# Attention after a scan layer: one copy of q and k for maxima and scores, two heads on the halves of the array, a written order per engine, projections in a stage of their own

## The chip, the cores and the metric

One Trainium2 chip, one core. The metric is device time in microseconds: 4778.94 us as the median of three runs of the kernel before (4752.04 to 4829.39).

## What is computed

Two layers over x of shape 8 x 1024 x 256 (batch, position, width), all in float32. The first is a selective scan with a gated convolution, followed by a layer norm. The second is attention with 16 heads of 16 channels plus a mixture of eight experts with the best two kept, followed by a layer norm. The change touches the attention alone.

```python
qkv = (x @ W_qkv + b_qkv).reshape(B, S, 3, H, hd)
q, k, v = (qkv[:, :, 0], qkv[:, :, 1], qkv[:, :, 2])
attn = jnp.einsum('bqhd,bkhd->bhqk', q, k) / jnp.sqrt(jnp.asarray(hd, x.dtype))
attn = jax.nn.softmax(attn, axis=-1)
attn_out = jnp.einsum('bhqk,bkhd->bqhd', attn, v).reshape(B, S, D)
...
return attn_out + moe_out
```

## The kernel before

`scan_moe_layer` does the whole first layer and the experts of the second. It leaves, per batch, the sum of x and the experts' part in DRAM (`acc`) and the transposed x (`x2T`). `attention_layer` then does the attention, batch by batch, in pairs of heads: 8 batches of 8 pairs, 64 pairs.

*Projections.* `prep(b, o)` (L596 on) projects one batch. Each block of 128 channels by 512 positions of q or k (`pq`, L614) is split into a high part, rounded to float32r by ACT (L619), and a low part by DVE (L620). Both go to DRAM (`qk`, L625), each block in two DMAs, so that q lies as (high, low, high, low) and k as (high, high, low, low): the product of 64 such rows is the full product of 16 channels. V goes to `vaug` (L634, L639) with a column of ones after each head. `prep(0)` runs before the loop; the following batches' preparations are generators whose pieces the loop puts between its own work.

*Maxima.* A softmax wants the maximum of every query's scores first. `maxima` (L664 to L703) multiplies with the queries as output rows: for each of 8 query tiles and 2 halves of the keys, two matmuls of 64 rows, one per head on each half of the array (`sm`, L689), then one DVE reduction over 1024 columns (L693). At the end of a pair, `insert` (L667 to L678) transposes the negated maxima (`pm`), splits them into high and low (L671, L672), and four small DMAs write them as two rows under q in `qst` (L675).

*Scores.* `score(n)` (L706 on) multiplies with the keys as output rows, 66 rows deep: 64 rows of k and two rows of ones meet 64 rows of q and the two rows of maxima, so the maximum is subtracted inside the product. One score tile is one head, 128 keys and 1024 queries: two matmuls (`sc`, L714), then one exponential of 1024 columns by ACT (L716). So q and k of a pair are loaded twice, into `qmx`, `kmx` for the maxima and `qst`, `kst` for the scores (L656, L662), in rings of three.

*Weighing.* `weigh(n)` (L720 on) multiplies V with the exponentials of two score tiles, four heads-by-halves side by side on strips of 32 columns (`av`, L733). After the last one ACT copies the result (L739); `collect` transposes it back (L747), divides by the sum of weights (L751, L754) and POOL adds it to `acc` (L758). `normalize` does the last layer norm of a batch on DVE (L765 to L776), the power on POOL (L772).

*Order.* TensorE (PE), ACT, DVE and POOL follow the order in which the program is written; SP, which issues the DMAs, is not among them. The loop at the end of `attention_layer` makes one step of maxima, a weighing in every second turn and one score tile per turn; the maxima run 24 steps (`LEAD`) ahead, 16 steps being a pair. Score and maxima tiles share three buffers of 1024 columns in PSUM, `ps_s`; the projections, transposes and the like have one, `ps_m`.

Of the kernel before, what the change touches and what calls it, by code (L numbers as in the profile page):

```python
# [47 lines left out]

# [475 lines left out]
@with_exitstack  # L534
def attention_layer(ctx, tc, ident, acc_in, x2T, w_qkv, b_qk, b_v, out):

# [10 lines left out]
    RING = 3  # L556
    LEAD = 24
    TILES = 2 * NT
    PIECES = 24
    VW = HD + 1  # L560

    wp = ctx.enter_context(tc.tile_pool(name="a_w", bufs=1))
    p1 = ctx.enter_context(tc.tile_pool(name="a_1", bufs=1))
    p2 = ctx.enter_context(tc.tile_pool(name="a_2", bufs=2))
    p3 = ctx.enter_context(tc.tile_pool(name="a_3", bufs=3))
    p5 = ctx.enter_context(tc.tile_pool(name="a_5", bufs=5))
    ps_s = ctx.enter_context(tc.tile_pool(name="a_pss", bufs=3, space=PSUM))
    ps_a = ctx.enter_context(tc.tile_pool(name="a_psa", bufs=1, space=PSUM))
    ps_m = ctx.enter_context(tc.tile_pool(name="a_psm", bufs=1, space=PSUM))
    dp = ctx.enter_context(tc.tile_pool(name="a_dram", bufs=2, space=DRAM))  # L570
# [8 lines left out]
    nc.gpsimd.memset(half, -0.5)  # L579

    vaug = []
    for i in range(2):
        t = wp.tile([P, NT, NH * VW + 32 - VW], F32, name=f"vaug{i}")
        nc.gpsimd.memset(t, 1.0)
        vaug.append(t)

    qmx, kmx, qst, kst = [], [], [], []
    for i in range(RING):
        qmx.append(wp.tile([P, S], F32R, name=f"qmx{i}"))
        kmx.append(wp.tile([P, S], F32R, name=f"kmx{i}"))  # L590
        qst.append(wp.tile([KS + 2, 2, S], F32R, name=f"qst{i}"))
        t = wp.tile([KS + 2, 2, S], F32R, name=f"kst{i}")
        nc.gpsimd.memset(t[KS : KS + 2].bitcast(F32), 1.0)
        kst.append(t)

    def prep(b, o):  # L596

        acc = p2.tile([P, NT, H], F32, tag="acc", name=f"acc_{b}")
        nc.sync.dma_start(acc, acc_in[b].rearrange("(t p) h -> p t h", p=P))
        o["acc"] = acc  # L600
        xT = p2.tile([P, HK, S], F32, tag="xT", name=f"axT_{b}")
        nc.sync.dma_start(xT, x2T[b])
        yield
        yield

        o["d"] = []
        for c in range(H // P):
            d = dp.tile([2, P, 2, 2, S], F32, tag=f"qk{c}", name=f"qk_{b}_{c}")
            o["d"].append(d)
            for a in range(2):  # L610
                for q in range(NQ):
                    pq = ps_m.tile([P, QB], F32, tag="mm", name=f"pq_{b}_{c}_{a}_{q}")
                    for k in range(HK):
                        nc.tensor.matmul(  # L614
                            pq, wr[:, k, a * H + c * P : a * H + (c + 1) * P], xT[:, k, q * QB : (q + 1) * QB],
                            start=(k == 0), stop=(k == HK - 1),
                        )
                    hl = p3.tile([P, 2, QB], F32R, tag="hl", name=f"hl_{b}_{c}_{a}_{q}")
                    nc.scalar.activation(hl[:, 0, :], pq, AF.Identity, bias=bqk[:, a, c : c + 1])  # L619
                    nc.vector.scalar_tensor_tensor(  # L620
                        hl[:, 1, :], pq, bqk[:, a, c : c + 1], hl[:, 0, :].bitcast(F32), ALU.add, ALU.subtract
                    )
                    for i in range(2):
                        dst = d[a, :, :, i, :] if a == 0 else d[a, :, i, :, :]
                        nc.sync.dma_start(dst[:, :, q * QB : (q + 1) * QB], hl.bitcast(F32))  # L625
                    yield
        va = vaug[b % 2]
        o["v"] = va
        for t2 in range(NT // 2):
            pv = ps_m.tile([P, 2, H], F32, tag="mm", name=f"pv_{b}_{t2}")  # L630
            for j in range(2):
                t = 2 * t2 + j
                for k in range(HK):
                    nc.tensor.matmul(  # L634
                        pv[:, j, :], xT[:, k, t * P : (t + 1) * P], wr[:, k, 2 * H :],
                        start=(k == 0), stop=(k == HK - 1),
                    )
            for j in range(2):
                nc.vector.tensor_add(  # L639
                    va[:, 2 * t2 + j, 0 : NH * VW].rearrange("p (h d) -> p h d", d=VW)[:, :, 0:HD],  # L640
                    pv[:, j, :].rearrange("p (h d) -> p h d", d=HD), bv.rearrange("p (h d) -> p h d", d=HD),
                )
            yield

    pairs = [(b, p) for b in range(NB) for p in range(NP)]
    work = [{} for _ in range(NB)]

    def rows_of(i, a):
        b, p = pairs[i]
        c, r = divmod(2 * p, HC)  # L650
        return work[b]["d"][c][a, HD * r : HD * r + 2 * HD].rearrange("d i j s -> (d i j) s")

    def load_max(i):
        if i < len(pairs):
            for a, t in ((0, qmx[i % RING]), (1, kmx[i % RING])):
                nc.sync.dma_start(t.bitcast(F32), rows_of(i, a))  # L656

    def load_pair(i):
        if i < len(pairs):
            for a, t in ((0, qst[i % RING]), (1, kst[i % RING])):  # L660
                for hh in range(2):
                    nc.sync.dma_start(t[0:KS, hh, :].bitcast(F32), rows_of(i, a)[KS * hh : KS * hh + KS])  # L662

    def maxima():  # L664


        def insert(i, mn):  # L667
            pt = ps_m.tile([P, P], F32, tag="mm", name=f"pm_{i}")
            nc.tensor.transpose(pt[:TILES, :], mn, ident)
            mr = p2.tile([TILES, 2, P], F32R, tag="mr", name=f"mr_{i}")  # L670
            nc.scalar.copy(mr[:, 0, :], pt[:TILES, :])  # L671
            nc.vector.tensor_sub(mr[:, 1, :], pt[:TILES, :], mr[:, 0, :].bitcast(F32))  # L672
            for hh in range(2):
                for l in range(2):
                    nc.sync.dma_start(  # L675
                        qst[i % RING][KS + l : KS + l + 1, hh, :].bitcast(F32),
                        mr[hh * NT : (hh + 1) * NT, l, :].bitcast(F32),
                    )  # L678

        mn = None  # L680
        for i, (b, p) in enumerate(pairs):
            qt_, kt_ = qmx[i % RING], kmx[i % RING]
            mh = p2.tile([P, 2, NT, NQ], F32, tag="mh", name=f"mh_{b}_{p}")
            for t in range(NT):
                for kh in range(NQ):
                    s = ps_s.tile([P, 2, QB], F32, tag="s", name=f"sm_{b}_{p}_{t}_{kh}")
# [7 lines left out]
                    if i and t == 1 and kh == 0:  # L694
                        insert(i - 1, mn)
# [5 lines left out]
        insert(i, mn)  # L701
        yield

    live = {}

    def score(n):  # L706

# [171 lines left out]
```

## Time and profile before

| | |
|---|---|
| median of the runs | 4778.94 us |
| runs | 4752.04 to 4829.39 us |
| profiled execution, span from first to last instruction | 4713.3 us |
| busy: PE, DVE, ACT, POOL | 4031.4, 3296.9, 2322.1, 1940.1 us |
| granted TensorE clock, mean | 0.896 |
| first projection of the attention | 2603.5 us |
| first exponential, last exponential | 2670.7, 4693.0 us |
| DMA | 454.6 MB, 96 GB/s |

Times are microseconds from the first instruction unless they are durations. PE is TensorE's matmuls, PEld its weight loads, DVE VectorE, ACT ScalarE, POOL GpSimd, SP the engine that issues DMAs. L693 is line 693 of the kernel. In a group, `out<-in` are the program's names, then the shape, the count, busy time and mean nanoseconds of one, and the engine's idle time before it with what ended most of it. A float32 matmul has two records, a float32r one has one. The profiled execution's own time outside its span isn't recorded; the median of the runs is 65.6 us above the span, the shortest run 38.7.

### The profile page before, as it was taken

To read this page: it belongs to the slowest core of one execution; us is meant where nothing else is said; L and a number is where in the kernel's file an instruction comes from. 1 tells how busy PE (TensorE), PEld (TensorE's weight loads), DVE (VectorE), ACT (ScalarE), POOL (GpSimd) and SP (SyncE) were. 2 spreads that over 40 slices of the span, in tenths; PEclk is the share of its full clock that TensorE was granted. 3 is DMA by queue.
4 is the path that set the end of the run, shared out by engine and by line. 5 is a ranking of instruction groups with operands and counts; after the bars stand their busy time and mean duration, and the time that the engine had idled before them with its cause. 6 is when DMAs were issued, how large, how long until landed. Compare 5 with 4: busy or idle time off the path is not lost.

```text
span 4713.3 us, 43473 instructions
## 1 busy us (share of the span) xinstructions
PE 4031.4 (86%) x15168; PEld 1528.1 (32%) x15168; DVE 3296.9 (70%) x3774; ACT 2322.1 (49%) x3178; POOL 1940.1 (41%) x664
## 2 busy tenths in 40 slices
PE   7688787887888878878766799999999999999998
PEld 2233332332233323333222233333333333333333
DVE  4777787677777777777783467567676666776765
ACT  4545444554455444534430156456565455555555
POOL 4978777787777776877781000000000000000000
PEclk8788898898988988899878799699999798998989
DMA  5433334333333433433321542243434242423321
GB/s 139 103 93 89 77 92 99 83 95 74 99 86 90 91 84 85 108 77 84 87 58 45 168 142 79 90 126 106 137 90 144 63 152 73 143 82 117 108 72 28
DMA packets 188621, 454.58 MB, mean 96 GB/s; under 512 B 25882, under 2 KB 63410, under 8 KB 187378
## 3 DMA queue, kind: packets, MB, share of 16 engines
q1 hardware_dynamic: 188402, 451.80, 35.4%
q8 instruction: 120, 1.97, 0.2%
q14 instruction: 99, 0.81, 0.1%
HBM read 323.78 MB, written 126.88 MB: 96 GB/s over the span
## 4 chain that ended last, share of the span: by engine, by line
PE 56%; DVE 17%; ACT 11%; POOL 6%; issue 4%; DMA 1%; ACTq 0%; POOLq 0%; SPq 0%; DVEq 0%
PE sc L714 12%; PE av L733 11%; PE pe L386 8%; PE sm L689 7%; ACT es L716 7%; DVE dz L493 6%; PE pc L191 5%; DVE x L394 5%; POOL dz L445 3%; DVE dz L438 3%; PE pq L614 2%; POOL dz L440 2%; PE pr L240 2%; PE y L455 1%; PE po L283 1%
## 5 line engine op out<-in xcount | busy, mean ns | idle before, releaser
L693 DVE TENSOR_REDUCE mh<-sm 128x2 f32<-128x1024 f32 x1024 | 1243.2, 1222 | 380.2 <-PE sm L689 372.0
L716 ACT ACTIVATE es<-sc 128x1024 f32<-128x1024 f32 x1024 | 1047.0, 1024 | 810.3 <-PE sc L714 783.8
L445 POOL TENSOR_TENSOR dz<-dz,ct 128x2048 f32<-128x2048 f32 x256 | 1156.6, 4524 | 504.1 <-DVE dz L493 264.3
L428 ACT ACTIVATE da<-ex,am 128x512 f32<-128x512 f32 x1024 | 700.0, 689 | 945.6 <-DVE dz L493 926.6
L714 PE MATMUL sc<-qst,kst 66*128 66x512 f32 x2048 | 796.9, 473 | 41.2 <-ACT es L716 36.4
L758 POOL TENSOR_TENSOR acc<-acc,ot 128x256 f32<-128x256 f32 x64 | 46.7, 729 | 1842.8 <-DVE ot L754 1720.8
L386 PE MATMUL pe<-we,yT 128*128 128x512 f32 x1024 | 528.2, 640 | 217.4 <-DVE x L394 214.2
L493 DVE TENSOR_TENSOR_SCAN dz<-da,state,dz 128x512 f32<-128x512 f32 x512 | 629.5, 1268 | 88.5 <-ACT da L428 87.3
L493 DVE TENSOR_TENSOR_SCAN dz<-da,dz 128x512 f32<-128x512 f32 x512 | 596.6, 1206 | 56.9 <-ACT da L428 56.6
L440 POOL TENSOR_TENSOR dz<-ex,bt 128x2048 f32<-128x2048 f32 x128 | 591.6, 4622 | 24.6 <-DMA ex<-dl 22.8
L733 PE MATMUL av<-es,vaug 128*32 128x512 f32 x4096 | 589.5, 649 | 0.0
L689 PE MATMUL sm<-kmx,qmx 64*128 64x512 f32 x2048 | 544.3, 528 | 29.1 <-DVE mh L693 7.7
L714 PEld LDWEIGHTS sc<-qst,kst 66*128 66x128 f32 x2048 | 325.6, 200 | 647.8 <-DVE mh L693 262.5
L394 DVE SCALAR_TENSOR_TENSOR x<-pe,gcb,x 128x256 f32<-128x256 f32 x512 | 246.4, 481 | 274.7 <-PE pe L386 265.5
L386 PEld LDWEIGHTS pe<-we,yT 128*128 128x128 f32 x1024 | 180.9, 195 | 547.3 <-issue 526.7
L689 PEld LDWEIGHTS sm<-kmx,qmx 64*128 64x128 f32 x2048 | 201.8, 194 | 458.9 <-ACT es L716 215.9
L455 PE MATMUL y<-dz,sl 128*32 128x512 f32 x2048 | 307.8, 677 | 42.7 <-POOL dz L445 42.7
L438 DVE TENSOR_TENSOR dz<-ex,pb 128x2048 f32<-128x2048 f32 x128 | 289.6, 2263 | 55.0 <-DMA ex<-dl 55.0
L191 PE MATMUL pc<-hs,dw 128*128 128x512 f32 x512 | 260.5, 646 | 45.2 <-POOL hs L182 45.2
L254 PE MATMUL pb<-xd,rp 16*128 16x512 f32 x256 | 154.7, 685 | 105.6 <-DVE dz L438 70.0
L171 PE MATMUL ph<-xT,wi 128*128 128x512 f32 x256 | 171.1, 807 | 63.3 <-DVE x L301 45.5
L240 PE MATMUL pr<-xT,wi 128*128 128x512 f32 x256 | 144.5, 715 | 32.3 <-ACT du L230 29.8
(104 smaller groups left out, 2816.7 us busy)
## 6 DMA issues: line engine op xcount, KB each, us to landing
ex<-dl SPq DMA_DIRECT2D x256, 512.0 KB
qk<-hl SPq DMA_DIRECT2D x128, 512.0 KB
dl<-du SPq DMA_DIRECT2D x64, 512.0 KB
qmx<-qk SPq DMA_DIRECT2D x64, 512.0 KB
kmx<-qk SPq DMA_DIRECT2D x64, 512.0 KB
qst<-qk SPq DMA_DIRECT2D x128, 256.0 KB
kst<-qk SPq DMA_DIRECT2D x128, 256.0 KB
ct<-bc SPq DMA_DIRECT2D x256, 64.0 KB
```

Of the source, the lines that this page charges most:

```text
L191: nc.tensor.matmul(pc, dw[:, c0 + j, k, :], hss[j][:, k : k + LT], start=(k == 0), stop=(k == KC - 1))
L386: nc.tensor.matmul(pe.rearrange("p e f -> p (e f)"), yT[:, k, t * P : (t + 1) * P], we[:, k, 2 * e2 : 2 * e2 + 2, :].rearrange("p e f -> p ...
L394: nc.vector.scalar_tensor_tensor(xt[:, t, :], pe[:, j, :], cb[:, t, e : e + 1], xt[:, t, :], ALU.mult, ALU.add)
L428: nc.scalar.activation(da, o["ex", c][:, r, 0, :], AF.Exp, scale=am[:, c, g, r : r + 1])
L440: nc.gpsimd.tensor_mul(t, o["ex", c][:, :, 1, :], o["bt", g].unsqueeze(1).to_broadcast(full))
L445: nc.gpsimd.tensor_mul(t, t, o["ct", g].unsqueeze(1).to_broadcast([P, NR, LT]))
L493: nc.vector.tensor_tensor_scan(t[:, r, :], da, t[:, r, :], 0.0 if steps[i][1] == 0 else state[:, c, g, r : r + 1], ALU.mult, ALU.add,)
L689: nc.tensor.matmul(s[:, hh, :], qt_[rows, t * P : (t + 1) * P], kt_[rows, kh * QB : (kh + 1) * QB], start=True, stop=True,)
L693: nc.vector.tensor_reduce(mh[:, :, t, kh], s, AX.X, ALU.max)
L714: nc.tensor.matmul(s[:, cols], kt_[:, hh, kt * P : (kt + 1) * P], qt_[:, hh, cols], start=True, stop=True)
L716: nc.scalar.activation(e, s, AF.Exp, scale=HD**-0.5)
L733: nc.tensor.matmul(av[32 * j : 32 * j + 32, :], va[:, kt, VW * h : VW * h + 32], es[hh][:, q * QB : (q + 1) * QB], start=(kt == 0), stop=( ...
```

## The change

One copy of q and of k per pair, `q4` and `k4` of 128 rows with one head on each half, serves maxima and scores alike, and each is loaded once. A score tile is now both heads for 128 keys and 512 queries: two matmuls of 64 rows on the halves, and then two more that add the maxima, `ones` (two rows of ones in each half, zeros elsewhere) against `mrow` (the two rows of maxima in each half, zeros elsewhere). A maxima tile has two buffers of one bank, each reduced by a DVE instruction of its own over 512 columns. DRAM holds q and k once (high and low); the copies arise in the loads.

The order is no longer a loop of generators. Every piece of work is a task with an engine, a duration that the plan assumes and a place `v` in that engine's order; one unit of `v` holds one tile of 128 queries of the maxima and one of 128 keys of the scores. On each engine the tasks are emitted sorted by `v`; the plan's clock decides buffers and the order on SP, which is now among the engines that follow the written order. Within a unit TensorE has, by `v`: the weighing, a maxima tile, two score tiles, a maxima tile. Once per pair the transposes of an older pair (`back`) and of the maxima (`turn`) stand between the two score tiles and share one score buffer. The maxima are 11 units ahead of the scores (`LEAD`), 8 units being a pair. PSUM buffers: two score tiles (`R_s`), three single banks for maxima and projections (`R_d`), one for the weighing.

All projections, in half batches, get places below zero, ahead of all pairs. Last, `normalize` scales on POOL, except for six of eight tiles of the last batch.

```diff
+class Plan:
+    ENGINES = ("PE", "ACT", "DVE", "POOL")
+    TAIL = {"PE": 0.3, "DVE": 0.17, "ACT": 0.2, "POOL": 0.12, "SP": 0.0}
+    SWITCH = 0.2
...
+    def add(self, eng, us, fn, v, reads=(), writes=(), mode=None):
+        t = Task()
+        t.eng, t.us, t.fn, t.v, t.mode = eng, us, fn, v, mode
+        t.tail = self.TAIL[eng]
...
+    def run(self):
+        from collections import deque
+        queue = {e: deque(sorted((t for t in self.tasks if t.eng == e), key=lambda t: (t.v, t.n))) for e in self.ENGINES}
+        sp = [t for t in self.tasks if t.eng == "SP" and not t.left]
+        free = dict.fromkeys(self.ENGINES + ("SP",), 0.0)
...
+            for t in [q[0] for q in queue.values() if q] + sp:
+                if t.left:
+                    continue
+                at = max(free[t.eng], t.ready)
+                taken = []
+                for b in t.new:
+                    if b.slot is None:
+                        j = b.pool.find(taken)
+                        if j is None:
+                            break
+                        at = max(at, b.pool.free[j])
+                        taken.append((b.pool, j))
+                else:
+                    if best is None or (at, t.v, t.n) < best[:3]:
+                        best = (at, t.v, t.n, t)
...
+            if e == "SP":
+                sp.remove(t)
+                free[e] = at + 0.06
+                dma = max(dma, at + 0.06) + t.us
+                t.end = dma + 2.0
+            else:
+                queue[e].popleft()
+                us = t.us
+                if e == "PE" and t.mode != mode:
+                    us += self.SWITCH
+                    mode = t.mode
+                free[e] = at + us
+                t.end = at + us + t.tail
+            t.fn()
...
-    RING = 3
-    LEAD = 24
-    TILES = 2 * NT
-    PIECES = 24
+    LEAD = NT + 3
+    LATE = 2
     VW = HD + 1
+    VR = NH * VW + 32 - VW
+    plan = Plan()
...
+    ones_in = wp.tile([P, P], F32, name="ones_in")
+    nc.sync.dma_start(ones_in, ones2)
+    ones = wp.tile([P, P], F32R, name="ones")
+    nc.scalar.copy(ones, ones_in)
+    R_v = ring("vaug", NB, [P, NT, VR])
+    for t in R_v.tiles:
         nc.gpsimd.memset(t, 1.0)
-        vaug.append(t)
-    qmx, kmx, qst, kst = [], [], [], []
-    for i in range(RING):
-        qmx.append(wp.tile([P, S], F32R, name=f"qmx{i}"))
-        kmx.append(wp.tile([P, S], F32R, name=f"kmx{i}"))
-        qst.append(wp.tile([KS + 2, 2, S], F32R, name=f"qst{i}"))
-        t = wp.tile([KS + 2, 2, S], F32R, name=f"kst{i}")
-        nc.gpsimd.memset(t[KS : KS + 2].bitcast(F32), 1.0)
-        kst.append(t)
-    def prep(b, o):
-        o["d"] = []
+    R_q = ring("q4_", 3, [P, S], F32R)
+    R_k = ring("k4_", 3, [P, S], F32R)
+    R_m = ring("mrow", 2, [P, S], F32R)
+    for t in R_m.tiles:
+        nc.gpsimd.memset(t.bitcast(F32), 0.0)
+    R_s = ring("s", 2, [P, 2, QB], pool=pp)
+    R_d = ring("d", 3, [P, QB], pool=pp)
+    R_av = ring("av", 1, [P, QB], pool=pp)
+    R_es = ring("es", 10, [P, 2, QB])
+    R_x = ring("axT", 2, [P, HK, QB])
+    R_avs = ring("avs", 2, [P, QB])
+    R_hl = ring("hl", 4, [P, 2, QB], F32R)
+    R_acc = ring("acc", 2, [P, NT, H])
+    R_mh = ring("mh", 2, [P, 2, NT, NQ])
+    R_mn = ring("mn", 2, [P, 2 * NT])
...
+    def prep(b, q, v0):
+        o, xT, n = work[b], Buf(R_x), 0
+        def load():
+            nc.sync.dma_start(xT.t, x2T[b][:, :, q * QB : (q + 1) * QB])
+        plan.add("SP", 3.0, load, v0 - 2, writes=[xT])
+                pq, hl = Buf(R_d), Buf(R_hl)
+                def proj(pq=pq, c=c, a=a):
                     for k in range(HK):
                         nc.tensor.matmul(
-                            pq, wr[:, k, a * H + c * P : a * H + (c + 1) * P], xT[:, k, q * QB : (q + 1) * QB],
+                            pq.t, wr[:, k, a * H + c * P : a * H + (c + 1) * P], xT.t[:, k],
                             start=(k == 0), stop=(k == HK - 1),
                         )
-                    hl = p3.tile([P, 2, QB], F32R, tag="hl", name=f"hl_{b}_{c}_{a}_{q}")
-                    nc.scalar.activation(hl[:, 0, :], pq, AF.Identity, bias=bqk[:, a, c : c + 1])
...
+                plan.add("PE", 1.71, proj, v, reads=[xT], writes=[pq], mode="f")
+                plan.add("ACT", 0.6, high, v, reads=[pq], writes=[hl])
+                plan.add("DVE", 0.65, low, v + 0.05, reads=[pq, hl], writes=[hl])
+                def store(hl=hl, c=c, a=a):
+                    nc.sync.dma_start(
+                        o["d"][c][a, :, :, q * QB : (q + 1) * QB].rearrange("i p s -> p i s"), hl.t.bitcast(F32)
+                    )
+                plan.add("SP", 2.5, store, v, reads=[hl], writes=[o["dbuf"][c]])
+        for t2 in range(TQ // 2):
+            v = v0 + 0.1 * n
+            n += 1
+            pv = Buf(R_d)
...
+            plan.add("PE", 1.71, projv, v, reads=[xT], writes=[pv], mode="f")
+            plan.add("DVE", 0.65, addv, v + 0.05, reads=[pv], writes=[o["v"]])
...
+        v0 = NT * i
+        q4, k4, mrow = Buf(R_q), Buf(R_k), Buf(R_m)
+        for a, t in ((1, k4), (0, q4)):
+            for hh in range(2):
+                def load(a=a, t=t, hh=hh):
+                    heads = o["d"][c][a, :, HD * (r + hh) : HD * (r + hh + 1)]
+                        dst = t.t[KS * hh + 2 * HD * i : KS * hh + 2 * HD * (i + 1)].bitcast(F32)
+                        src = heads if a == 0 else heads[i : i + 1].to_broadcast([2, HD, S])
+                        nc.sync.dma_start(dst, src)
+                plan.add("SP", 1.5, load, v0 - 4, reads=[o["dbuf"][c]], writes=[t])
+        mh, mn, mr = Buf(R_mh), Buf(R_mn), Buf(R_mr)
+        for t in range(NT):
+            for kh in range(NQ):
+                s = [Buf(R_d), Buf(R_d)]
+                v = v0 + t + (0.2, 0.8)[kh]
+                def mx(s=s, t=t, kh=kh):
                     for hh in range(2):
                         rows = slice(KS * hh, KS * hh + KS)
                         nc.tensor.matmul(
-                            s[:, hh, :], qt_[rows, t * P : (t + 1) * P], kt_[rows, kh * QB : (kh + 1) * QB],
+                            s[hh].t, q4.t[rows, t * P : (t + 1) * P], k4.t[rows, kh * QB : (kh + 1) * QB],
-                    nc.vector.tensor_reduce(mh[:, :, t, kh], s, AX.X, ALU.max)
-                    if i and t == 1 and kh == 0:
-                        insert(i - 1, mn)
-                    yield
-            mn = p2.tile([P, TILES], F32, tag="mn", name=f"mn_{b}_{p}")
-            nc.vector.tensor_reduce(mn.rearrange("p (h t) -> p h t", h=2), mh, AX.X, ALU.max, negate=True)
-            load_max(i + RING)
-        yield
...
+                    plan.add("DVE", 0.585, red, v, reads=[s[hh]], writes=[mh])
+        v = v0 + NT
+        pm = Buf(part_of=seam.setdefault(i, Buf(R_s)))
...
+        def turn():
+            nc.tensor.transpose(pm.t[: 2 * NT, 0, 0:P], mn.t, ident)
...
+        plan.add("DVE", 0.1, neg, v - 0.1, reads=[mh], writes=[mn])
+        plan.add("PE", 0.12, turn, v + 1.51, reads=[mn], writes=[pm], mode="f")
+        plan.add("ACT", 0.2, high, v + 1.52, reads=[pm], writes=[mr])
+        plan.add("DVE", 0.2, low, v + 1.21, reads=[pm, mr], writes=[mr])
+        for hh in range(2):
+            for l in range(2):
+                def row(hh=hh, l=l):
+                    nc.sync.dma_start(
+                        mrow.t[KS * hh + l : KS * hh + l + 1, :].bitcast(F32),
+                        mr.t[hh * NT : (hh + 1) * NT, l, :].bitcast(F32),
+                    )
+                plan.add("SP", 0.05, row, v, reads=[mr], writes=[mrow])
+        av = Buf(R_av)
+        for kt in range(NT):
+            es = []
+            for q in range(NQ):
+                s, e = Buf(R_s), Buf(R_es)
+                es.append(e)
+                v = v0 + LEAD + kt + (0.4, 0.6)[q]
+                cols = slice(q * QB, (q + 1) * QB)
+                def score(s=s, kt=kt, cols=cols):
+                    for hh in range(2):
+                        rows = slice(KS * hh, KS * hh + KS)
+                        nc.tensor.matmul(
+                            s.t[:, hh, :], k4.t[rows, kt * P : (kt + 1) * P], q4.t[rows, cols], start=True, stop=False
+                        )
+                    for hh in range(2):
+                        rows = slice(KS * hh, KS * hh + KS)
+                        nc.tensor.matmul(s.t[:, hh, :], ones[rows, :], mrow.t[rows, cols], start=False, stop=True)
...
+                plan.add("PE", 0.43, score, v, reads=[q4, k4, mrow], writes=[s], mode="h")
+                plan.add("ACT", 0.93, exp, v, reads=[s], writes=[e])
...
+            plan.add(
+                "PE", 0.92, weigh, v0 + LEAD + kt + LATE, reads=[o["v"], *es, *([av] if kt else [])],
+                writes=[av], mode="c",
+            )
+        v = v0 + LEAD + NT - 1 + LATE
+        avs, pt, rc, ot = Buf(R_avs), Buf(part_of=seam.setdefault(i + 3, Buf(R_s))), Buf(R_rc), Buf(R_ot)
+        w = v0 + 4 * NT
...
+        plan.add("ACT", 0.5, out_av, v + 0.35, reads=[av], writes=[avs])
+        plan.add("PE", 0.45, back, w + 1.5, reads=[avs], writes=[pt], mode="f")
+        plan.add("DVE", 0.2, recip, w + 1.22, reads=[pt], writes=[rc])
...
+            plan.add("DVE", 0.22, scale, w + 1.23, reads=[pt, rc], writes=[ot])
...
+            def norm(t=t):
+                eng = nc.vector if last and t % 4 else nc.gpsimd
+                eng.tensor_scalar(
+                    acc.t[:, t, :], acc.t[:, t, :], mv.t[:, t, 0:1], rs.t[:, t : t + 1], ALU.subtract, ALU.mult
+                )
+            plan.add("DVE" if last and t % 4 else "POOL", 0.7, norm, v0 + gap * (NT + t), reads=[mv, rs, acc], writes=[acc])
...
+            prep(b, q, NQ * b + q - 20)
+    for b in range(NB):
+        load_acc(b)
+        for p in range(NP):
+            pair(b * NP + p)
+        normalize(b)
-    with tc.manual_schedule(engines={eng.PE, eng.Activation, eng.DVE, eng.Pool}):
-        mx = maxima()
-        for _ in range(LEAD):
-            step(mx)
-        gens, due = [], 0.0
...
-            step(mx)
-            if n % 2 == 0 and 0 <= n - 4 < ALL:
-                weigh(n - 4)
-            if n < ALL:
-                score(n)
...
+    with tc.manual_schedule(engines={eng.PE, eng.Activation, eng.DVE, eng.Pool, eng.SP}):
+        plan.run()
```

## The prediction

> **What bounds the kernel now.** I read the page's busy times and slices first, then its groups by line, then the timeline of a quiet stretch, then the busy times by window. A unit below means two maxima tiles, two score tiles and one weighing; 8 units make a pair of heads, and there are 64 pairs.
>
> ```profile
> span 4713.3 us, 43473 instructions
> PE   7688787887888878878766799999999999999998
> PEclk8788898898988988899878799699999798998989
> L693 DVE TENSOR_REDUCE mh<-sm 128x2 f32<-128x1024 f32 x1024 | 1243.2, 1222 | 380.2 <-PE sm L689 372.0
> L716 ACT ACTIVATE es<-sc 128x1024 f32<-128x1024 f32 x1024 | 1047.0, 1024 | 810.3 <-PE sc L714 783.8
> ```
>
> The attention is the right half of the slices: from about 2600 us on TensorE is at 9 in nearly every one. The maxima (DVE, L693) and the exponentials (ACT, L716) idle, both because of TensorE. The timeline shows one unit, start to start:
>
> ```profile
> 3404.30 0.73 PE L714 MATMUL sc<-qst,kst 66*128 66x512 f32 x2
> 3405.11 0.51 PE L689 MATMUL sm<-kmx,qmx 64*128 64x512 f32 x2
> 3405.55 1.07 PE L733 MATMUL av<-es,vaug 128*32 128x512 f32 x8
> 3406.55 0.73 PE L714 MATMUL sc<-qst,kst 66*128 66x512 f32 x2
> 3407.21 0.50 PE L689 MATMUL sm<-kmx,qmx 64*128 64x512 f32 x2
> 3407.64 0.73 PE L714 MATMUL sc<-qst,kst 66*128 66x512 f32 x2
> ```
>
> Score 0.81 (0.15 of it a wait for an exponential's buffer), maxima 0.44, weighing 1.00, score 0.66, maxima 0.43: 3.34 us. The single records at full clock give the same, as medians: a maxima pair 0.425, a score tile 0.337 + 0.326, a weighing 0.453 + 0.542, together 3.17. How much of that is streaming? A 512-column pass takes 0.2155 (a projection of V, two passes of 256 columns per record, repeats every 0.2155; Q and K records every 0.428). So a maxima pair, whose two matmuls start 2 ns apart, streams 0.21 and loses 0.21; a score tile streams 0.43 and loses 0.23; the weighing streams 0.853 and loses 0.14. Five visits lose 1.04 us of 3.34.
>
> A clean pair takes 27.2 us, yet the 64 take 2022 (4693 less 2671), 31.6 each. The rest is projections put in between, and the clock:
>
> ```profile
> 2604.00:2648.00 44.00, 27.62 (x78) 12.54 (x76) 14.02 (x21) 5.50 (x8) 2.68 (x2) 0.97 0.80 270
> 2648.00:2671.00 23.00, 16.29 (x43) 6.05 (x41) 22.96 (x23) 0.59 (x2) 0.00 (x0) 0.50 0.79 213
> 2671.00:2706.00 35.00, 34.70 (x93) 11.58 (x91) 15.59 (x15) 13.17 (x14) 0.00 (x0) 0.50 0.09 32
> 2948.00:3020.00 72.00, 72.00 (x211) 23.68 (x211) 34.61 (x41) 27.11 (x29) 2.39 (x2) 0.50 0.16 44
> 3020.00:3700.00 680.00, 649.31 (x3138) 248.61 (x3138) 489.15 (x573) 395.94 (x423) 20.09 (x25) 1.00 0.39 122
> ```
>
> The columns after the length are PE, PEld, DVE, ACT and POOL, then the clock, the DMA share and GB/s. Some stretches run at a clock of 0.50 though TensorE never rests; 284 us between 2671 and 4693 do, and a unit is 6.46 there.
>
> **The change, part by part.** (1) *One mode for maxima and scores.* A score tile becomes two pairs of half-height matmuls (the scores, then the row of ones against the maxima), each pair as wide as a maxima pair. Streaming does not shrink: 4 passes before, 4 after. What falls is visits: the written order is weighing, maxima, score, score, maxima, so two visits instead of five. Six pairs in a row cost 0.2155 each at best and 0.235 by the closest row (three maxima pairs in a row at 2641.39 come 0.338 and 0.235 apart, the first with its entry); I take 0.22, since the trace's last units put four score matmuls in a row into 1.13 us, which leaves 0.225 each after 0.23 for the visit. Unit: 6 x 0.22 + 0.23 entry and exit + 0.995 = 2.55 (2.52 to 2.64). The 0.15 wait goes: ACT needs 2 x 1.03 of 2.55.
>
> (2) *Maxima per bank.* Each 1024-wide reduction becomes two of 512. Back to back the wide one repeats every 1.137 us (14 in 15.92 from 2645.09). No 512-wide reduction is in the trace: half of it is 0.57, and the 128x512 additions record 0.67. Records overlap by 0.09 (1.222 against 1.137), so I take 0.60, nearest to the addition less that overlap. DVE per unit: 2.40 (2.27 to 2.68), under the 2.55 of TensorE but close.
>
> The Trainium skill (TensorEngine Tiling (Array Packing), Performance Considerations) speaks against the change here: tiling speeds up TensorE and not the emptying of PSUM. By that rule with the upper price, 2.68, DVE would set the unit and a pair would be 24.7; by the row it does not.
>
> (3) *The seam of each pair.* Transposes, which were spread out, now stand together once per pair between two score tiles: four at 0.108, an exit of 0.20, the turn of the maxima 0.21 and one more entry and exit of the half mode 0.23, about 1.0 us on TensorE. They take one of two score buffers. By hand, with the durations above: from the start of the unit the first score ends at 1.8, the transposes at 2.65; ACT is free for the copy of the maxima at 3.1; the second score waits for the first exponential until 3.15, the next weighing starts at 4.05. So a seam costs 1.5. DVE, behind that copy, runs the correction, reciprocal and two scalings until 4.45 and is level again one unit later. Queued behind it are the reductions of the second maxima tile, and TensorE waits for these only through three banks, which just suffices.
>
> (4) *Maxima rows by DMA.* From seam start: the first copy ends at 3.4 and the second at 3.65, four issues of 0.64 on SP follow; at 3303.04 to 3307.13 first issue to last packet took 4.1. That makes 7.5; the ones pass needs the rows at 8.1, three units of lead instead of the four before. 0.6 to spare, nothing in the sum beyond the 0.6 below. If SP is in the middle of the next pair's eight loads (0.5 each), the rows are 3.4 to 5 late.
>
> (5) *Loads.* 1 MB a pair instead of 2, eight issues of 0.5 against six: SP is off the path. Nothing gained; these lay beside TensorE.
>
> (6) *Projections in their own stage.* Per half batch 4 x 1.71 + 2 x 1.72 = 10.3, sixteen times 164.6, plus 1.7 for a first window at half clock and 4 for edges: 170. With three buffers for a chain of 3.6 us (1.71, then 0.3, 0.69, 0.75 and waits) TensorE keeps going; with one, as before, the cadence was 3.55 and the stage 320, the upper bound. The moved DMAs are 64 stores of 512 KB (32 us of SP issue) and 16 loads: 42 MB, which at the 270 GB/s of the window above is 155 us, under 165; at 213 GB/s it is 197 and the stage 27 longer. All pair loads now queue on SP behind these stores, which costs the first pair alone, and its data are ready early.
>
> (7) *Normalising* moves to POOL, which idles, except at the end; statistics stay, 0.57 of DVE a pair.
>
> Per pair: TensorE 8 x 2.55 + 1.0 = 21.4; DVE 8 x 2.40 + 1.2 + 0.57 = 21.0. I take 8 x 2.55 + 1.5 seam + 0.6 for what DVE does not fit + 0.6 for rows and semaphores = **23.1** (21.4 to 25.5).
>
> (8) *Clock.* I laid the records of matmul columns over the clock's windows of 3.41 us. In windows at half clock, the 99 after which it rose were covered 0.81 or more in 19 of 20 (median 0.89); of the 188 after which it stayed, three quarters were at 0.82 or less. At full clock, windows after which it held had 0.50 or more in 19 of 20; those after which it fell, 0.46 or less in three of four. The old unit at half clock covers 4.27 of 6.46, 0.66, and it rose only where projections ran. The new one covers 4.27 of 4.83 (0.88), and 2.13 of 2.55 at full. The lead, eleven units of maxima alone at 2.40, will drop it; I price the way back at 10 us (a 35 us stretch like 2671 to 2706 loses 17, a single window 2).
>
> The Trainium skill (TensorE: Matmul & The Clock Gate, Part 1) has the clock rise after one busy window of about 3.4 us. The 72 us at half clock above, busy throughout, do not agree. By the page the way back is 2 us and the sum 8 less.
>
> Sum: first projection 2603.5 as before (it waits for weights loaded after 2597) + 170 + lead 11 x 2.40 = 26.4 + clock 10 + 64 x 23.1 = 1478 - 5 (last eleven units without maxima at 2.11) + tail 20 as before = **4303**, 410 under 4713.3. The median of the runs is 65.6 above the profiled span; kept, that is **4369 us**.
>
> **Rivals.** *Rows late on SP*: each pair loses 5, a pair is 28, span 4617, time 4683. For: 0.6 to spare. Against: the pair loads wait for the score tile behind the seam, so rows come first. *Halves that do not overlap when they accumulate*: a score tile is four passes in a row, unit 2 x 0.22 + 8 x 0.2155 + 0.23 + 0.995 = 3.39, +430, time 4800, no change. This is also the case of a change that does not do what it says. Against: maxima pairs start together, and nothing in the trace shows passes adding into one bank to be slower. *The clock stays at half* (slower): the lead drops it, no projection lifts it any more, a pair is 8 x 4.83 + 2.5 = 41.1. For: windows at 0.91 that stayed are in the trace. Against: 0.88 is the median of those that rose. All through, +1152, time 5520; from 28 pairs of 64 on it makes the kernel over 2% slower. *Waits all vanish*: pair at or under 21.1, time 4240 or less.
>
> **How the numbers follow.** Forecast 0.75, own range 4260 to 4520 (pairs of 21.4 to 25.5); rows late 0.07; no overlap 0.05; half clock 0.08; floor 0.05. The range 4230 to 4640 holds the forecast, most of the late rows and a little of the floor. Two per cent is about what a measurement of this kernel can tell from no change. Faster by more: 0.75 + 0.05 + 0.04 of the late rows = 0.84; within: 0.05 + 0.03 = 0.08; slower 0.08.
>
> **What would show it.** Right: half-mode matmuls in runs of six pairs 0.22 apart, units of 2.5 to 2.7, DVE over 0.85 busy, a clock of 1.0 after the lead, projections done near 2773. Wrong: a score tile above 0.5, TensorE waiting for the maxima rows or for DVE in every unit, reductions of 0.67 apart, or long stretches at 0.50.

## The result and the profile after

The changed kernel takes 4982.48 us (median of four runs, 4968.28 to 4984.81) against 4786.38 for the kernel before: 1.0424 times its time, 95% interval 1.0379 to 1.0469. It is slower, where 4369 was forecast. Ratios here are of undisturbed runs alone and need not be those of the medians.

The page of the changed kernel, its span, three slices of time, and the groups of the maxima, the exponentials and the maxima's matmuls:

```profile
span 4983.1 us, 48690 instructions
PE   7688887878878788788665977777777777777777
PEclk8788899988999889998777888888888888888888
DMA  5433333333333334333114500110101010101010
L835 DVE TENSOR_REDUCE mh<-d 128x1 f32<-128x512 f32 x2048 | 1286.9, 684 | 681.1 <-PE d L826 675.2
L889 ACT ACTIVATE es<-s 128x1024 f32<-128x1024 f32 x1024 | 999.7, 1022 | 1068.1 <-PE s L886 1059.8
L826 PE MATMUL d<-k,q 64*128 64x512 f32 x2048 | 627.5, 503 | 459.5 <-DMA q<-qk 378.1
...
```

TensorE, at 9 in nearly every slice of the attention before, is at 7, and it idles for a DMA: 378 us before the maxima, for the load of q. Before, the maxima's matmuls had waited 0.3 us for one:

```profile
L689 PE MATMUL sm<-kmx,qmx 64*128 64x512 f32 x2048 | 544.3, 528 | 29.1 <-DVE mh L693 7.7 <-DMA qst<-qk 0.3
```

DVE and ACT idle longer than before, still behind TensorE. The clock is 0.86 throughout the pairs. And the DMA engines, on which the maxima wait, are busy a tenth of the time. The list of waits, for the projections' stage (2597 to 2840) and for the pairs (2870 to 4960), gives total, number and longest:

```profile
ACT hl L752 <- DMA qk<-hl: 61.0, 3, 58.6
...
PE d L826 <- DMA q<-qk: 378.1, 94, 4.7
```

The stage stops once, 58.6 us long, for a store to DRAM; then every pair waits for its q. The stop first: SP's next store, and the end of ACT's wait for it:

```profile
2685.48 4.95 SPq L765 DMA_DIRECT2D qk<-hl  x2
...
2702.98 0.69 ACT L752 ACTIVATE hl<-d,bqk 128x512 fp32r<-128x512 f32 x1 [58.56 <-DMA qk<-hl]
```

The block that this store takes was ready at 2636.6. From 2635.38 to 2685.4 SP was issuing the 24 loads of the first three pairs, 50 us in all: the first in 0.6 to 0.8 us each, most in 2.3 to 3.1. So about 41 us of the stop are a store that SP had not issued, and 17.5 the time from its issue until it had landed. A wait for q in the timeline, with SP's issues of that pair's loads at the top:

```profile
3518.77 2.83 SPq L814 DMA_DIRECT2D k<-qk  x4
3521.65 4.74 SPq L814 DMA_DIRECT2D q<-qk  x4
...
3532.35 0.52 PE L826 MATMUL d<-k,q 64*128 64x512 f32 x2
3532.80 1.06 PE L898 MATMUL av<-es,vaug 128*32 128x512 f32 x8
3537.05 0.46 PE L826 MATMUL d<-k,q 64*128 64x512 f32 x1 [3.18 <-DMA q<-qk]
3542.09 0.76 PE L826 MATMUL d<-k,q 64*128 64x512 f32 x1 [4.58 <-DMA q<-qk]
```

The loads are issued from 3518.77 on, 15.1 us before they are wanted at 3533.86, where the weighing ends, and they end at 3541.5: the first head's maxima start at 3537.05, the second's at 3542.09. A pair takes 33.4 us on average; a unit is 2.70 outside the seam (4.03), the stop and the half clock around it. The packets tell how the load runs. From 3520.2 to 3541.5 the 256 packets of 4 KB (1 MB) go two at a time: for 20.4 us exactly two are under way. So eight loads of 128 KB use two DMA engines, 2.5 us a load, and the share of 0.10 to 0.12 of sixteen engines is two of them nearly full. The records name no engine; that they are two is read from these counts. In the kernel before, 2.1 MB between 3329 and 3336 went mostly sixteen at a time.

What differs is the order in which a load walks its source. Before, the rows lay in DRAM as they were wanted and a load walked 64 or 128 rows. Now its source is `heads`, two parts (high and low) of 16 channels: the slowest dimension has 2 steps. The Trainium skill states the rule (DMA: Bandwidth & Descriptors, Why a DMA increments its semaphore by 16 and not by 1): a DMA is split over the largest number of engines, up to 16, that divides the slowest dimension of both sides. The trace agrees: two at a time.

**Theory.** The loads run on two DMA engines, and that alone turns a faster kernel into a slower one. **Rivals.** A: k's rows are read twice (the source repeats), and that is slow. B: eight issues on SP, or their place behind the four small rows of the maxima, are late. C: the order or the half-mode matmuls are what is slow.

### The profile page after: what moved, and what is told of

It is laid out like the page before. It is cut to its first block, busy times and chain, and to the rows that moved or that the text cites. A ratio compares the mean times of both kernels' runs of the same rounds, so it can differ in the third digit from the quotient of the medians.

```text
span 4983.1 us, 48690 instructions
## 1 busy us (share of the span) xinstructions
PE 3852.0 (77%) x17216; PEld 1682.4 (34%) x17216; DVE 3333.7 (67%) x4700; ACT 2267.6 (46%) x3179; POOL 2020.7 (41%) x735
## 4 chain that ended last, share of the span: by engine, by line
PE 40%; DMA 24%; DVE 14%; POOL 7%; SPq 5%; ACT 5%; issue 5%; POOLq 0%; ACTq 0%; DVEq 0%
DMA q<-qk 22%; PE pe L375 8%; DVE dz L482 5%; PE av L898 5%; PE pc L180 5%; PE d L826 5%; SPq L814 4%; DVE x L383 4%; POOL dz L434 4%; PE s L881 3%; DVE dz L427 3%; PE s L886 3%; POOL dz L429 2%; PE d L746 2%; PE pr L229 2%
## 5 line engine op out<-in xcount | busy, mean ns | idle before, releaser
L835 DVE TENSOR_REDUCE mh<-d 128x1 f32<-128x512 f32 x2048 | 1286.9, 684 | 681.1 <-PE d L826 675.2
L889 ACT ACTIVATE es<-s 128x1024 f32<-128x1024 f32 x1024 | 999.7, 1022 | 1068.1 <-PE s L886 1059.8
L826 PE MATMUL d<-k,q 64*128 64x512 f32 x2048 | 627.5, 503 | 459.5 <-DMA q<-qk 378.1
L826 PEld LDWEIGHTS d<-k,q 64*128 64x128 f32 x2048 | 318.2, 201 | 1011.7 <-issue 517.5
L881 PE MATMUL s<-q,k 64*128 64x512 f32 x2048 | 499.2, 440 | 31.7 <-ACT es L889 31.7
L886 PE MATMUL s<-mrow,ones 64*128 64x512 f32 x2048 | 477.5, 423 | 0.0
L881 PEld LDWEIGHTS s<-q,k 64*128 64x128 f32 x2048 | 245.7, 207 | 81.8 <-ACT es L889 59.1
L886 PEld LDWEIGHTS s<-mrow,ones 64*128 64x128 f32 x2048 | 257.4, 207 | 45.5
```

The source lines that it names most:

```text
L826: nc.tensor.matmul(s[hh].t, q4.t[rows, t * P : (t + 1) * P], k4.t[rows, kh * QB : (kh + 1) * QB], start=True, stop=True,)
L835: nc.vector.tensor_reduce(mh.t[:, hh, t, kh : kh + 1], s[hh].t, AX.X, ALU.max)
L881: nc.tensor.matmul(s.t[:, hh, :], k4.t[rows, kt * P : (kt + 1) * P], q4.t[rows, cols], start=True, stop=False)
L886: nc.tensor.matmul(s.t[:, hh, :], ones[rows, :], mrow.t[rows, cols], start=False, stop=True)
L889: nc.scalar.activation(e.t, s.t, AF.Exp, scale=HD**-0.5)
```

## The experiments

**Channels first** (`e1_sixteen`). The same eight loads of 32 rows, the same repeated reading, walked the other way, so that the slowest dimension is 16. q and k rows change places alike.

```diff
                         src = heads if a == 0 else heads[i : i + 1].to_broadcast([2, HD, S])
+                        src = src.rearrange("j d s -> d j s")
                         nc.sync.dma_start(dst, src)
```

> The changed kernel with one line more: each load of q and k keeps its 32 rows of 4 KB, but its source is walked channel first, then high and low, so the slowest dimension is 16 and not 2. Theory (a load whose slowest dimension is 2 runs on two DMA engines, 128 KB in 2.5 us and the eight of a pair in 22.6): the eight then take under 5 us, TensorE's wait of 9 us per pair for q goes, and so does the 58 us stop among the projections; pair 24.3, span 4983 - 62 x 9 - 58 = about 4365. Rival A (the repeated reading of k's rows is what is slow, not the spread): k's loads stay as slow, pair 29 or more, span above 4700. Rival B (eight issues on SP, and where they stand behind the maxima rows, are too late): little changes, span above 4850.

Measured: 4310.75 us (4307.9 to 4312.03), 0.9161 of the kernel before, interval 0.9031 to 0.9291, span 4308.0. The fastest of the seven runs of the kernel before beside these took 4677.46 us, 365 more than the slowest of these. One line changes a kernel that is 4% slower into one that is 8% faster. Rivals A and B are out: the repeated reading, the eight issues and their place are still there. (SP was held up as well, but by the slow loads: the 24 loads that took it 50 us in the stage of the changed kernel take 15.8 here.) The page's slices, then its maxima:

```profile
PE   7688788788888787878887667999999999999998
PEclk8689989998898998898898788999999999999999
L836 DVE TENSOR_REDUCE mh<-d 128x1 f32<-128x512 f32 x2048 | 1273.9, 682 | 82.1 <-PE d L827 76.6
```

TensorE is at 9 again, at full clock, and DVE's idle time before the maxima falls from 681 to 82 us. A pair takes 23.16 on average, 22.9 to 24.5 but for the last. The eight loads now take 5.3 us from first to last packet (3506.26 to 3511.54), mostly between six and sixteen packets at a time. The gain over the changed kernel is 675 us, more than the 618 expected, and a wait's cost in clock is the likely rest: in the changed kernel 7 to 10 us at half clock go with every stop, of which 3.2 to 6.5 lie after its end (5.1 on average); here there is none from 2815 to 4297.

**Twice the issues** (`e2_issues`). Channels first, each load in two halves of its columns.

```diff
-                        nc.sync.dma_start(dst, src)
+                        for n in range(2):
+                            cols = slice(n * QB, (n + 1) * QB)
+                            nc.sync.dma_start(dst[:, cols], src[:, :, cols])
```

> The loads of e1 with channels first, each cut into two halves of the columns: 16 issues a pair for 8, packets of 2 KB for 4 KB. Theory (engines, not issues): as e1 within 20 us, about 4365 to 4385, since 16 issues of 0.6 us are 10 us of SP in a pair of 24. Rival B (issues on SP set the time): 5 us more per pair than e1, over 300 us slower than e1.

Measured: span 4326.2, one run. The pairs are the same to the tenth (23.16 on average); the 18 us are all at the start, where the first exponential is at 2830.0 for 2812.0 (the scan ends 5 us later, and the stage of projections is 13 longer). SP's issues don't set the pairs.

**More time for the slow loads** (`e3_ring4`). Two engines as in the changed kernel, but a fourth buffer and an earlier place.

```diff
-    R_q = ring("q4_", 3, [P, S], F32R)
-    R_k = ring("k4_", 3, [P, S], F32R)
+    R_q = ring("q4_", 4, [P, S], F32R)
+    R_k = ring("k4_", 4, [P, S], F32R)
-    R_es = ring("es", 10, [P, 2, QB])
+    R_es = ring("es", 8, [P, 2, QB])
-                plan.add("SP", 1.5, load, v0 - 4, reads=[o["dbuf"][c]], writes=[t])
+                plan.add("SP", 1.5, load, v0 - 12, reads=[o["dbuf"][c]], writes=[t])
```

> The changed kernel with its loads as they are (slowest dimension 2), but four buffers each for q and k instead of three and the loads asked for 8 units earlier (eight buffers of exponentials instead of ten, to make room). Theory: the eight loads still take 22.6 us of two engines, but have a whole pair of 24.3 us more to arrive; the wait for q goes nearly, pair 24.5 to 26, span 4400 to 4520, since the stop at the start remains and has one more pair of loads in it (80 us). If loads were not slow but held up by something on SP ahead of them, the extra buffer would bring little: pair 31 or more, span above 4800.

Measured: span 4426.1, inside the range; pair 24.0 on average, 23.0 in most. The eight loads, 21 us, fit in a pair of 23 if they may start a pair earlier. What remains are six longer pairs of 29 to 31 us, one in a batch, and their waits, the first of them with what SP did before it:

```profile
PEld s L886 <- DMA mrow<-mr: 40.0, 7, 7.5
```

```profile
3150.79 0.28 DVE L853 TENSOR_TENSOR mr<-s,mr 16x128 fp32r<-16x128 f32 x1 [0.43 <-ACT mr L850]
3156.20 0.37 SPq L944 DMA_DIRECT2D acc<-acc_d  x1
3156.66 2.83 SPq L863 DMA_DIRECT2D mrow<-mr  x4
3161.60 1.16 PE L886 MATMUL s<-mrow,ones 64*128 64x512 f32 x2 [5.60 <-DMA mrow<-mr]
```

Seven times the scores wait for the maxima rows, six of them 5.6 us and more, each in one of the long pairs. The rows were ready at 3151.1, but SP issued them at 3156.66, behind the load of `acc`, which stands ahead of them in the written order and waits until an output store has landed (65.2 us of such waits in the pairs, the longest 11.0; in `e1_sixteen` 15.7 and 2.9). That store's packets show what held it: of the 1024 of the output's two stores there, 896 had started by 3148.8, and the last 128, two sixteenths, started from 3153.07 on, when the loads' last packets had ended. All six waits look alike; this is read from the trace and was not tried by itself. The stage of projections takes 246 us: here SP is at 32 loads for 70 us, and ACT waits 79.0 us for the store behind them.

**The slow loads in the kernel before** (`e4_before_two`). Rows of q and k in another order, even rows first, then odd.

```diff
-                nc.sync.dma_start(t.bitcast(F32), rows_of(i, a))
+                for hh in range(2):
+                    rows = slice(KS * hh, KS * hh + KS)
+                    src = rows_of(i, a)[rows].rearrange("(x two) s -> two x s", two=2)
+                    nc.sync.dma_start(t[rows].bitcast(F32), src)
...
-                    nc.sync.dma_start(t[0:KS, hh, :].bitcast(F32), rows_of(i, a)[KS * hh : KS * hh + KS])
+                    src = rows_of(i, a)[KS * hh : KS * hh + KS].rearrange("(x two) s -> two x s", two=2)
+                    nc.sync.dma_start(t[0:KS, hh, :].bitcast(F32), src)
```

> The kernel before, with the rows of every q and k load in another order (the even rows, then the odd, alike for q and k), so that the slowest dimension of each load's source is 2; 2 MB a pair as before, eight issues for six. Theory: at 1 MB in 22.6 us a pair needs 45 us of two DMA engines where it took 31.6, so the span grows by 64 x 13.5 = 860 or a little more, to 5550 to 5750. Rival (what slowed the changed kernel is its order or its reading of rows twice, not the number of engines): within 50 us of the kernel before, 4713.

Measured: 5649.57 us, span 5647.9, one run; a pair takes 44.8 us where 45 was expected from 2 MB at the rate of the changed kernel. Of the 45 us from 3500 on, exactly two packets of the loads are under way for 40.0. The cost has moved into a kernel without any other part of the change, so rival C is out. Its largest wait of TensorE for a DMA is for the small maxima rows:

```profile
PE sc L718 <- DMA qst<-mr: 415.0, 46, 13.9
```

Of the 32 packets of 512 bytes that carry a pair's rows, 24 start within 2 to 3 us and the last eight, in most pairs, 9 to 13 us after the first; in the kernel before all 32 start within 2.7. So a quarter of a pair's packets stands behind the loads.

**Four steps** (`e5_four`). Loads of 16 rows, walked in four groups of four.

```diff
-                        dst = t.t[KS * hh + 2 * HD * i : KS * hh + 2 * HD * (i + 1)].bitcast(F32)
-                        src = heads if a == 0 else heads[i : i + 1].to_broadcast([2, HD, S])
-                        src = src.rearrange("j d s -> d j s")
-                        nc.sync.dma_start(dst, src)
+                        for j in range(2):
+                            row = KS * hh + 2 * HD * i + HD * j
+                            src = heads[j] if a == 0 else heads[i]
+                            nc.sync.dma_start(
+                                t.t[row : row + HD].bitcast(F32), src.rearrange("(y x) s -> x y s", x=4)
+                            )
```

> The loads once more, each of 16 rows now (16 issues a pair), with the source walked in four groups of four rows, so that the slowest dimension is 4. Theory (as many DMA engines as the slowest dimension has steps): four packets of 4 KB under way at a time, 1 MB at twice the rate of the changed kernel, 11 us a pair instead of 22.6; that hides in a pair, 23.2 to 23.5, and only the start is later: 4326 (the 16 issues with channels first) plus 0 to 30. Rival (any order other than channels first is slow, whatever the count): waits for q come back, pair above 28, span above 4600.

Measured: span 4320.4; pairs 23.16. Between 3500 and 3524 four packets of the loads are under way for 9.9 us and five or more for 0.6: slowest dimension 2, 4 and 16 give two, four and up to sixteen packets at a time. At four engines the loads are hidden. The 0 to 30 us of a later start didn't come.

The parts of the change, on top of the line of `e1_sixteen`:

**Projections back among the pairs** (`e6_spread`). The two places of `0.1 * n` in `prep` take the gap as well.

```diff
-            prep(b, q, NQ * b + q - 20)
+            if b == 0:
+                prep(b, q, q - 20)
+            else:
+                prep(b, q, NT * NP * (b - 1) + 4.9 + 24 * q, 4.0)
```

> Channels-first loads, and of the change's three parts one undone: the projections of batches 1 to 7 stand among the pairs of the batch before again, a piece of 1.71 us every fourth unit, behind the second maxima tile. Theory (a stage of their own saves only the visits and the borrowed banks): the stage shrinks by 7 x 20.6 = 144 us, and each of the 84 pieces costs 1.71 plus a visit of 0.25 and up to 1.5 us of waits for a bank and for DVE and ACT: +164 to +290, net +20 to +145 on 4308. Rival (the stage of its own is what the gain comes from, since the clock stays up only so): half clock in many pairs, span above 4500.

Measured: span 4346.3, 38 more than with the stage. The stage shrinks from 178 to 34 us, and a pair with two pieces takes 27.1 for 23.0, so a piece costs 2.06: 84 of them 173. The clock stays up: no half clock from 2682 to 4334. The rival is out; the stage of its own is worth about 38 us of some 400. The rest lies in the pairs: units of 2.70 for 3.34, and no half clock, where the kernel before has 284 us of it between 2671 and 4693. How much each brings was not tried apart.

**One more visit** (`e7_visits`). A visit is a stretch of matmuls in one tile mode. The weighing of a unit in two halves of its columns, the first between the two score tiles.

```diff
-                "PE", 0.92, weigh, v0 + LEAD + kt + LATE, reads=[o["v"], *es, *([av] if kt else [])],
-                writes=[av], mode="c",
+                    "PE", 0.46, weigh, v0 + LEAD + kt + LATE - 0.5 + 0.5 * n,
+                    reads=[o["v"], *es, *([av] if kt or n else [])], writes=[av], mode="c",
```

> Channels-first loads, and the weighing of a unit in two visits, the first 256 columns between the two score tiles and the rest where it was: the same streaming, two visits more per unit. Theory (a visit costs entry and exit; 0.14 for the weighing, 0.32 for the half mode by the records of the changed kernel): 0.47 a unit, 0.35 where TensorE waits 0.12 for a bank anyway, 512 units: +180 to +240 us, 4490 to 4550. Rival (the visits cost little, the gain over the kernel before comes from the clock alone): within 40 us of 4308.

Measured: span 4541.7, 234 more; a unit takes 3.21 for 2.71, 0.50 for the two visits more (one of each mode). A unit of TensorE in each kernel shows it, first with one visit per mode, then with two:

```profile
3508.61 0.51 PE L827 MATMUL d<-k,q 64*128 64x512 f32 x2
3508.94 0.40 PE L882 MATMUL s<-q,k 64*128 64x512 f32 x2
3509.17 0.40 PE L887 MATMUL s<-mrow,ones 64*128 64x512 f32 x2
3509.41 0.39 PE L882 MATMUL s<-q,k 64*128 64x512 f32 x2
3509.64 0.39 PE L887 MATMUL s<-mrow,ones 64*128 64x512 f32 x2
3509.87 0.52 PE L827 MATMUL d<-k,q 64*128 64x512 f32 x2
3510.31 1.07 PE L899 MATMUL av<-es,vaug 128*32 128x512 f32 x8
```

```profile
3502.81 0.78 PE L827 MATMUL d<-k,q 64*128 64x512 f32 x2
...
3503.99 0.64 PE L902 MATMUL av<-es,vaug 128*32 128x256 f32 x8
3504.56 0.50 PE L882 MATMUL s<-q,k 64*128 64x512 f32 x2
3504.90 0.40 PE L887 MATMUL s<-mrow,ones 64*128 64x512 f32 x2
3505.14 0.39 PE L827 MATMUL d<-k,q 64*128 64x512 f32 x2
3505.46 0.64 PE L902 MATMUL av<-es,vaug 128*32 128x256 f32 x8
```

Within a visit the pairs start 0.23 apart; the first pair of a visit takes 0.34, and from the last pair to the weighing it is 0.32 to 0.44. Two visits more cost 234 of the some 400 us, and the change saves three of five: fewer visits are the larger part of what it gains by.

**The last projections in the lead** (`e8_lead`).

```diff
-            prep(b, q, NQ * b + q - 20)
+            if b < 7:
+                prep(b, q, NQ * b + q - 20)
+            else:
+                prep(b, q, 0.9 + 6 * q, 1.0)
```

> Channels-first loads, and the last batch's projections taken out of the stage and put among the first eleven units, in which there are maxima alone and TensorE rests for two thirds of the time. Theory: the stage is 20.6 us shorter, the lead a little longer for banks shared with the maxima; 5 to 18 us gained, 4290 to 4303, and the clock may stay up in the lead. Rival (banks: the maxima wait for the projections' three): the lead grows by as much, 4308 to 4325.

Measured: 4324.2 us (4321.79 to 4324.65), 0.9003 of the kernel before, interval 0.8956 to 0.905. The runs beside it were on another chip than those of `e1_sixteen`, so the two ratios are not compared with each other. In its own trace, from the first projection to the first exponential it is 217 us, against 207 in `e1_sixteen`: nothing is gained, and the rival is right. TensorE alternates, and the maxima wait for a bank that holds a projection:

```profile
2781.02 0.50 PE L827 MATMUL d<-k,q 64*128 64x512 f32 x2
2782.71 1.10 PE L827 MATMUL d<-k,q 64*128 64x512 f32 x2 [1.18 <-DVE hl L755]
2783.90 3.53 PE L746 MATMUL d<-axT,wr 128*128 128x512 f32 x4
```

The version that beats both kernels is `e1_sixteen`, by one line; the later projections of `e8_lead` are not needed for it.

## Why the prediction was wrong

The step that failed is (5), the loads. It counted bytes (half of before) and issues on SP, found both off the path and put them at nothing. It named no duration for a load of 128 KB of this form, though no load with such a source is in the trace of before, and gave no bound for it. The measured term is 22.7 us from first issue to last packet of a pair, of which 15.1 were covered: two stops of TensorE, 7.8 us together, more by the clock, 10.2 a pair in all, and 48 us in the stage. In (6) the same gap: the stores were reckoned against the bandwidth of sixteen engines, and the first pairs' loads behind them on SP were put down to the first pair alone. In truth three pairs' loads took SP 50 us, the stores came behind them, and the stage took 226 us for 170.

No rival and no part of the chances had slow loads; the whole 0.08 for slower stood on the clock. The rival of late rows had the right kind of event (a pair of 28 for want of a transfer) and the wrong transfer. Its reason was SP's queue; what was slow is the load itself.

With the loads spread, the rest of the sum can be read against `e1_sixteen`. The span is 4308.0, the sum was 4303, and some terms met by errors that cancel:

| term | predicted | measured in `e1_sixteen` |
|---|---|---|
| unit | 2.55 | 2.70 |
| seam unit | 4.05 | 4.03 |
| allowances in a pair (DVE, rows, semaphores) | 1.2 | about 0.2 |
| pair | 23.1 | 23.16 |
| reductions, start to start | 0.60 | 0.60 |
| stage | 170 | 178 |
| lead | 26.4 | 28.7 |
| clock after the lead | 10 | under 1 |

(1) Streaming and visits: right in kind (`e7_visits`), small in size by 0.15 a unit, 77 us in all. Pairs in a row are 0.233 apart and not 0.22, as three maxima pairs of the old trace had said, and the half mode loses 0.32 a visit and not 0.23. (2) was right. (3) came out to 0.02 by errors that cancel: over a unit of 2.70 the seam costs 1.33 and not 1.5. The allowances took the place of the missing 0.15: with DVE at 2.48 in a unit of 2.70 its extra work fits in. That the sum met the span of `e1_sixteen` to 5 us is in part luck. (4) Rows: TensorE waits for them once, 0.2 us. (8) The clock falls in the lead, as said, and is back 3.5 us after the first exponential (half clock from 2788 to 2815.5, first exponential at 2812.0), about one window of 3.41; the first pair takes 23.7. The rival of a clock that stays at half did not come, not even in the changed kernel, where it falls in every pair and rises again.

The conversion was wrong as well. The 65.6 us were taken for what lies around a span. A run of the changed kernel takes 1.7 us more than its span (4984.81 and 4983.1). The kernel before just runs unevenly: spans from 4675.7 to 4834.2 in later runs, at a mean clock of 0.905 and 0.869. `e1_sixteen` runs within 5 us (4307.9 to 4312.03), the changed kernel within 17.

## What to carry to other kernels

Before a load is put at nothing, look at the slowest dimension of both its sides, and not only at its bytes: 128 KB took 2.5 us with 2 steps there and 0.66 on average with 16 (eight in 5.3), and swapping two dimensions of the source was worth 675 us. A tenth of DMA share next to an engine that waits for a DMA was here a transfer on two of sixteen engines; counting how many packets are under way at once shows it. Where TensorE changes its tile mode, count visits: here two visits more cost 0.5 us of a unit of 2.7.

## What the runs showed of the hardware that was not expected

A slow load harms others in two ways. It holds the engine that issues it: in the stage of the changed kernel SP took 50 us for 24 loads, against 15.8 in `e1_sixteen`, and a store that was ready stood behind them for some 49 us. And a transfer that is spread wide ends late when a part of it stands behind the slow loads: two sixteenths of an output store in `e3_ring4`, a quarter of the packets of the maxima rows in `e4_before_two`, where TensorE waited 415 us for them.

A wait costs more than its length: with each stop of some 8 us the clock fell to half 3 to 5 us after the stop began in most pairs, and stayed there for 3.2 to 6.5 us after it had ended.

Half-height pairs in a row start 0.233 us apart, where full-height passes of 512 columns took 0.2155 by the records of the projections. Why is open.
